# Graph attention layer on one core: edge rows behind tile 1, the first product split at token 256, and splits and output sums moved to later places

## The chip, the core and the metric

The kernel runs on one core of one Trainium2 chip, in float32 (matrix products in the fp32r form). The metric is the device time of one execution in microseconds (us); several executions are summarised by their median. Engines are named as in the profile: PE is TensorE (PEld its weight loads), DVE is VectorE, ACT is ScalarE, POOL is GpSimd, and SP is SyncE, whose queue (SPq) issues nearly all DMAs.

## The reference, cut to what matters

```python
# N=384 tokens, D=1024 features, H=16 heads of 64
h = maximum(layernorm(x), 0)
q, k, v = h @ wq.T + bq, h @ wk.T + bk, h @ wv.T + bv
q2, k2, v2 = q @ wiq.T + biq, k @ wik.T + bik, v @ wiv.T + biv      # split into 16 heads
mask = -inf; mask[src, dst] = softplus(edge_weight)[type - 1]       # 6528 edges, last one wins; diagonal filled
attn = softmax(q2 @ k2.T / 8 + mask)
out  = x + (attn @ v2 as N x 1024) @ wo.T + bo
```

## The kernel before, in words

**Precision scheme.** Each float32 operand is split into a high part (fp32r) and a low remainder. A product is three matrix products: hi x hi, hi x lo, lo x hi. For a weight this means two instructions per chunk of 128 x 1024: `split_hi` (L77, a copy on ACT) and `split_lo` (L82, a subtraction on DVE or POOL).

**Weight stream.** The weights come as 56 chunks, numbered by `w`: 0-7 are wv, 8-15 wq, 16-23 wiv, 24-31 wk, 32-47 alternate wiq and wik (one pair `p` holds two heads), 48-55 are wo. `W0` is 32. `load(w)` (L62-L65) issues the DMA of a chunk into a tile `raw`, and there are three such buffers (`bufs=3`), so chunk `w` takes the buffer of chunk `w-3` once both splits of that one have read it. The split pair lies in `whl`, four buffers.

**Order.** The whole order is written out by hand (`manual_schedule`): every engine executes its instructions in the order in which the Python code emits them, and semaphores are put in by the framework. SP issues DMAs in that order as well.

**Start.** The three token tiles of x, the edge rows `er`, and the first weights are loaded (L95-L106). Each x tile goes through statistics (`ln_bn`, L251, DVE; `ln_mean`), subtraction of the mean (`ln_sub`, L280 ACT, L282 POOL, L284 DVE), transposition on PE (`ln_transpose`, L292), and a split into hi and lo (`ln_hi` L298 ACT, `ln_lo` L303 DVE). Chunk 0 is split on POOL in halves (L344, L346). `key_rows` (L180) turns the edge rows into keys on POOL and stores them to DRAM (L185); `key_load` (L196) reads them back, broadcast. The product of chunk 0 (L414) takes all hi x hi first, then halves of the low terms.

**Projections.** `proj` (L405) makes vT, qT and kT, L503 makes the values; the edge mask is built beside them on DVE, POOL and by DMA.

**Attention.** `fill_qk` (L593) is a generator of the wiq and wik products: per chunk `w` eight blocks of three matmuls into `gps[w]`, and a head task `qk_head(w)` (L576) that is to load chunk `w+4`, split chunk `w+2`, and evict the product before (`qk_done`, L548: ACT L377, DVE L378, then four DMAs that stack the result into `qs`, L557-L560, or `ks`, L567; for `p` above 0 all four are on SP). The first 28 blocks are emitted ahead of the loop (`PRE`), so the heads of chunks 32 to 35 too, with `now[0]` at -1. Then a loop of 59 steps (L767): step `i` emits, between filler blocks, the scores of head-tile `i` (`do_S`, L694, PSUM tag `s` with two banks), the masked maximum of `i-1` (`do_ttr`, L700, DVE, which frees the bank), the exponential of `i-2` (ACT L704), the normalisation of `i-3` (DVE L708, POOL L709), the transposes of `i-5` (L714), the split of the probabilities of `i-6` (L723, L724), every third step the value product (L731) and its eviction (L741, L742, L746, L747), and last the head tasks. Below, S6 stands for the scores of step 6; S0 to S5 use pair `p=0`, S6 is the first that needs `p=1`.

**Output.** When `fill_qk` is used up, `fill_o` (L657) fills the steps with the output product: for each of six output blocks the first half over four wo chunks (`KH`), whose sum is added to the residual by `ysum` (L651, L654, DVE), then the second half. `wo_prep(k)` (L623) splits wo chunk `k` at the steps in `WSTEPS`; `OPOOL` names the chunks whose low part POOL makes.

The head task before the change, which the text below follows instruction by instruction:

```python
def qk_head(w):
    first = w - W0 < 3
    if not first:
        load(w + 4)
        split_hi(w + 2)
    if pendq:
        pendq.pop(0)()
    if 0 < w - W0 < NTAB:
        mask_select(w - W0)
    if first:
        split_hi(w + 2)
    split_lo(w + 2, nc.gpsimd if (w + 2) % 2 == PAR else None)
```

## Time and profile before

| | |
|---|---|
| median of 3 runs | 303.34 us (301.37 to 303.49) |
| profiled execution, its own time | 302.19 us |
| its span, first to last instruction | 300.5 us (1.7 us lie around it) |
| PE busy | 293.1 us, 98% of the span |
| DVE, ACT, POOL busy | 200.5, 154.9, 155.7 us |
| granted TensorE clock | 0.999 |

The page of the profile gives busy time per engine, the span in 40 slices, the DMA queues, the chain of waits that ended last, and the costliest groups of instructions. The timeline lists instructions in order of time: start, duration, engine, line, operation, output<-input, and in brackets the idle time ahead of it with what ended it. A PE instruction's end is modelled, so between two matmuls the distance of their starts is the safer measure: in this trace it is 173 ns for 384 columns, 120 ns for 256 and 227 ns for 512.

### The profile page before, as it was taken

The numbers are of one execution on the slowest core, as the hardware profiler recorded it, in microseconds if no ns is written. First come the engines' busy times: TensorE is split into PE (matmuls) and PEld (weight loads), VectorE is DVE, ScalarE is ACT, GpSimd is POOL, SyncE is SP. The second block draws the span as 40 slices with busy tenths as digits, with TensorE's granted clock in tenths as the row PEclk, the third lists the DMA queues.
The fourth block names the chain that finished last, engine by engine and source line by source line (L and its number), as shares of the span: only waits on it lengthen the run. The fifth ranks groups of instructions, "written<-read, shape, count | busy, mean of one in ns | idle before, by whom it ended". The sixth has DMA issues, their size and how long they took to land.

```text
span 300.5 us, 4961 instructions
## 1 busy us (share of the span) xinstructions
PE 293.1 (98%) x1649; PEld 276.1 (92%) x1649; DVE 200.5 (67%) x492; ACT 154.9 (52%) x289; POOL 155.7 (52%) x164
## 2 busy tenths in 40 slices
PE   7899999999999999999999999999999999999995
PEld 5699999999988889999999999999999998888884
DVE  2959986655956463788865576767576757696523
ACT  3874644333422213554325667777777767676310
POOL 5865766271555785730033737373746467566210
PEclk9999999999999999999999999999999999999999
DMA  7899754642686668475369997646565636910005
GB/s 233 284 297 381 281 164 171 228 143 70 217 238 224 193 217 242 142 274 198 115 169 244 217 221 173 166 127 180 155 170 139 174 81 174 381 41 0 2 0 209
DMA packets 22377, 55.12 MB, mean 183 GB/s; under 512 B 4816, under 2 KB 8400, under 8 KB 22352
## 3 DMA queue, kind: packets, MB, share of 16 engines
q1 hardware_dynamic: 19968, 52.42, 57.7%
q0 software_dynamic: 2064, 1.80, 2.0%
q10 hardware_dynamic: 320, 0.59, 0.8%
q8 instruction: 13, 0.21, 0.3%
q14 instruction: 12, 0.10, 0.1%
HBM read 40.39 MB, written 4.97 MB: 151 GB/s over the span
## 4 chain that ended last, share of the span: by engine, by line
PE 95%; DMA 2%; DVE 1%; ACT 0%; issue 0%; SPq 0%
PE g L369 21%; PE g L367 21%; PE g L368 21%; PE s L694 6%; PE a L731 6%; PE t L714 5%; PE s L369 2%; PE s L368 2%; PE s L367 2%; DMA g<-in_x_dram 2%; PE t L369 2%; PE t L367 2%; PE t L368 2%; PE g L414 1%; PE a L369 1%; PE a L367 1%
## 5 line engine op out<-in xcount | busy, mean ns | idle before, releaser
L367 PE MATMUL g<-g,whl 128*128 128x384 f32 x312 | 106.4, 341 | 0.0
L369 PE MATMUL g<-g,whl 128*128 128x384 f32 x312 | 104.5, 335 | 0.0
L368 PE MATMUL g<-g,whl 128*128 128x384 f32 x312 | 104.2, 334 | 0.0
L228 POOL DMA_INDIRECT tab<-val,idx x51 | 57.6, 1129 | 40.3 <-issue 11.3
L77 ACT ACTIVATE whl<-raw 128x1024 fp32r<-128x1024 f32 x51 | 53.4, 1051 | 31.7 <-PE g L369 20.1
L709 POOL TENSOR_TENSOR e<-e,s 128x384 f32<-128x384 f32 x48 | 39.2, 830 | 41.2 <-DVE s L708 32.9
L368 PEld LDWEIGHTS g<-g,whl 128*128 128x128 f32 x312 | 58.7, 188 | 0.0
L367 PEld LDWEIGHTS g<-g,whl 128*128 128x128 f32 x312 | 58.6, 188 | 0.0
L369 PEld LDWEIGHTS g<-g,whl 128*128 128x128 f32 x312 | 58.5, 188 | 0.0
L82 DVE TENSOR_TENSOR whl<-raw,whl 128x1024 fp32r<-128x1024 f32 x41 | 50.2, 1224 | 9.6 <-ACT whl L77 7.9
L82 POOL TENSOR_TENSOR whl<-raw,whl 128x1024 fp32r<-128x1024 f32 x11 | 26.5, 2412 | 35.6 <-ACT whl L77 31.8
L383 ACT ACTIVATE g<-f,bc 128x384 fp32r<-128x384 f32 x24 | 14.8, 618 | 53.1 <-DVE f L382 46.8
L704 ACT ACTIVATE e<-e,s 128x384 f32<-128x384 f32 x48 | 29.4, 612 | 13.0 <-DVE s L700 13.0
L724 DVE TENSOR_TENSOR pt<-t,pt 128x384 fp32r<-128x384 f32 x48 | 26.4, 550 | 13.9 <-ACT pt L723 13.3
L723 ACT ACTIVATE pt<-t 128x384 fp32r<-128x384 f32 x48 | 23.2, 484 | 13.9 <-PE t L714 13.3
L700 DVE CUSTOM_DVE_ANT_0 e<-s,ma 128x384 f32<-128x384 f32 x48 | 26.3, 550 | 2.0 <-PE s L694 1.8
L694 PE MATMUL s<-ks,qs 128*128 128x384 f32 x96 | 25.3, 344 | 0.3 <-DVE s L700 0.2
L714 PE MATMUL t<-ident,e 128*128 128x128 f32 x144 | 23.5, 271 | 0.0
L382 DVE TENSOR_TENSOR f<-g,rrow 128x384 f32<-128x384 f32 x24 | 13.3, 555 | 13.5 <-PE g L369 7.6
L714 PEld LDWEIGHTS t<-ident,e 128*128 128x128 f32 x144 | 18.8, 140 | 3.1
L378 DVE SCALAR_TENSOR_TENSOR nat<-g,bc,nat 128x384 fp32r<-128x384 f32 x16 | 9.9, 618 | 16.4 <-ACT nat L377 14.4
L731 PE MATMUL a<-pt,vhl 128*128 128x384 f32 x96 | 20.8, 351 | 0.0
(147 smaller groups left out, 414.8 us busy)
## 6 DMA issues: line engine op xcount, KB each, us to landing
ks<-nat SPq DMA_DIRECT2D x30, 192.0 KB
raw<-in_wv_dram SPq DMA_DIRECT2D x8, 512.0 KB
raw<-in_wq_dram SPq DMA_DIRECT2D x8, 512.0 KB
raw<-in_wiv_dram SPq DMA_DIRECT2D x8, 512.0 KB
raw<-in_wk_dram SPq DMA_DIRECT2D x8, 512.0 KB
raw<-in_wiq_dram SPq DMA_DIRECT2D x8, 512.0 KB
raw<-in_wik_dram SPq DMA_DIRECT2D x8, 512.0 KB
raw<-in_wo_dram SPq DMA_DIRECT2D x8, 512.0 KB
```

Of the source, the lines that this page charges most:

```text
L77: nc.scalar.activation(dst[0], raw[w], AF.Copy)
L82: (eng or nc.vector).tensor_tensor(lo, raw[w], hi.bitcast(F32), OP.subtract)
L228: nc.gpsimd.indirect_dma_start(out=tabs[c // RNG], out_offset=bass.IndirectOffsetOnAxis(ap=idx[:, c:c + 1], axis=0), in_=val[:, c:c + 1], ...
L367: nc.tensor.matmul(ps, lhi, rhi, start=first, stop=False)
L368: nc.tensor.matmul(ps, lhi, rlo, start=False, stop=False)
L369: nc.tensor.matmul(ps, llo, rhi, start=False, stop=last)
L694: nc.tensor.matmul(ps[:, :N], qs[:, o, t * 128:(t + 1) * 128], ks[:, o, s, :], start=(s == 0), stop=(s == 1))
L704: nc.scalar.activation(es[i], es[i], AF.Exp, bias=s[:, 0:1], scale=-1.0, accum_out=s[:, 1:2])
L709: nc.gpsimd.tensor_tensor(es[i], es[i], s[:, 2:3].to_broadcast([128, N]), OP.mult)
L714: nc.tensor.transpose(ps[:, k * 128:(k + 1) * 128], es[i][:, k * 128:(k + 1) * 128], ident)
L724: nc.vector.tensor_tensor(lo, pv, hi.bitcast(F32), OP.subtract)
L731: nc.tensor.matmul(ps[:, :N], vhl[:, k, p, 2 * o:2 * o + 2, :], pts[h][:, s, k, :], start=(k == 0 and s == 0), stop=(k == 2 and s == 1))
```

## The change

Five edits: the DMA of the edge rows goes behind x tile 1 instead of tile 0; `key_rows`, `load(2)` and the first `key_load`s are emitted behind the mean subtraction of tile 0; the hi x hi product of chunk 0 is done first for tokens 0-255 and then for 256-383; in the heads of chunks 35 and 36 the splits of chunks 37 and 38 are taken out and emitted some steps later (`defer`), while load and eviction stay; and `ysum` of the first half is emitted behind `do_ttr` of its step (`ysums`, `flush_y`), with wo chunk 4's low part on POOL.

```diff
     for t in range(NT):
         nc.sync.dma_start(xt[t], x[t * 128:(t + 1) * 128, :])
-        if t == 0:
+        if t == 1:
             nc.sync.dma_start(er, erows)
...
-    key_rows()
-    load(2)
-    for s in range(NTAB):
-        key_load(0, s)
     ln_bn(0, 0)
     ln_bn(0, 1)
     ln_mean(0)
     ln_sub(0, 0, 512, nc.scalar)
     ln_sub(0, 512, D, nc.gpsimd)
+    key_rows()
+    load(2)
+    for s in range(NTAB):
+        key_load(0, s)
     p0 = ln_transpose(0)
...
             if w == 0:
-                for a, b, ks in ((0, 0, range(KT)), (1, 0, range(4)), (0, 1, range(4)), (1, 0, range(4, KT)),
-                                 (0, 1, range(4, KT))):
+                al = (0, N)
+                for a, b, ks, (n0, n1) in ((0, 0, range(KT), (0, 256)), (0, 0, range(KT), (256, N)),
+                                           (1, 0, range(4), al), (0, 1, range(4), al), (1, 0, range(4, KT), al),
+                                           (0, 1, range(4, KT), al)):
                     for k in ks:
-                        nc.tensor.matmul(ps[:, :N], whl[0][a][:, k * 128:(k + 1) * 128], src[:, b, k, :],
-                                         start=(a == b == k == 0), stop=(b == 1 and k == KT - 1))
+                        nc.tensor.matmul(ps[:, n0:n1], whl[0][a][:, k * 128:(k + 1) * 128], src[:, b, k, n0:n1],
+                                         start=(a == b == k == n0 == 0), stop=(b == 1 and k == KT - 1))
...
+    defer = []
+
+    def qk_split(w):
+        split_hi(w)
+        split_lo(w, nc.gpsimd if w % 2 == PAR else None)
+
     def qk_head(w):
         first = w - W0 < 3
         if not first:
             load(w + 4)
+            if w - W0 < 5:
+                pendq.pop(0)()
+                defer.append((now[0] + 6 - w + W0, w + 2))
+                return
             split_hi(w + 2)
...
-    PAR, OPOOL, ODVE = 1, (2, 3, 6), (2,)
+    PAR, OPOOL, ODVE = 1, (2, 3, 4, 6), (2,)
...
+    ysums = []
+
+    def flush_y():
+        while ysums:
+            ysum(ysums.pop(0))
+
     def fill_o():
...
             if k == 0:
+                flush_y()
                 oacc[OT[a]] = bank("g")
             omm(*OT[a], k)
             if k == KH - 1:
-                ysum(a)
+                ysums.append(a)
...
             if k == KH:
+                flush_y()
                 oacc[OT[a]] = bank("gggss"[a])
...
         if 0 <= i - 1 < S:
             do_ttr(i - 1)
+        flush_y()
...
         run_tasks()
+        while defer and defer[0][0] <= i:
+            qk_split(defer.pop(0)[1])
```

## The prediction

> **What bounds the kernel now.** I read the page first, then the chain of waits, then the timeline of the three stretches that the edits touch.

> The page's busy times (engine, us, share, instructions):

> ```profile
> PE 293.1 (98%) x1649; PEld 276.1 (92%) x1649; DVE 200.5 (67%) x492; ACT 154.9 (52%) x289; POOL 155.7 (52%) x164
> ```

> PE sets the time; no edit takes a matmul away (one adds eight). So I listed the distances between matmul starts and looked for those above the usual one of the shape. Between 19 and 165 us there is none. Gaps are left in four places: before the first product (12.26 us); S3 (0.15 + 0.11 us) and S6 (0.23 + 0.07); S15 and S21 (0.22 each), where nothing is changed; S44 and S45 (0.40 + 0.11, 0.15 + 0.11). **All that the change can win lies here: 0.57 us at S3 and S6, 0.77 at S44 and S45, and what comes off the start.**

> The start. First lines of the chain of waits (start, us, what), then rows of the timeline:

> ```profile
> 1.72 5.41 DMA g<-in_x_dram
> 7.16 1.30 DVE lnt L251 x2
> 12.26 4.41 PE g L414 x24
> ```

> ```profile
> 11.51 0.66 PE L292 MATMUL a<-ident,g 128*128 128x128 f32 x4
> 12.20 0.60 ACT L298 ACTIVATE g<-a 128x512 fp32r<-128x512 f32 x1
> 14.20 2.41 POOL L82 TENSOR_TENSOR whl<-raw,whl 128x1024 fp32r<-128x1024 f32 x1
> ```

> Tile 1 of x is waited for until 7.16; PE's last transposes of tile 2 start at 11.51, and the product waits until ACT has evicted them. The third row is weight chunk 1's low part, done at 16.61, first needed by PE at 16.85.

> Around S3 and S6, the timeline by engine:

> ```profile
> 159.71 2.49 POOL L82 TENSOR_TENSOR whl<-raw,whl 128x1024 fp32r<-128x1024 f32 x1 [3.76 <-ACT whl L77]
> 162.35 1.06 ACT L77 ACTIVATE whl<-raw 128x1024 fp32r<-128x1024 f32 x1 [2.26 <-DMA raw<-in_wiq_dram]
> 163.32 0.56 ACT L377 ACTIVATE nat<-g,bc 128x384 fp32r<-128x384 f32 x1
> 164.45 1.21 DVE L82 TENSOR_TENSOR whl<-raw,whl 128x1024 fp32r<-128x1024 f32 x1
> 165.58 0.55 DVE L700 CUSTOM_DVE_ANT_0 e<-s,ma 128x384 f32<-128x384 f32 x1
> 162.88 0.53 SPq L65 DMA_DIRECT2D raw<-in_wiq_dram  x1
> 164.56 2.64 SPq L567 DMA_DIRECT2D ks<-nat  x4
> 166.19 0.62 PE L694 MATMUL s<-ks,qs 128*128 128x384 f32 x2
> 172.08 0.58 PE L694 MATMUL s<-ks,qs 128*128 128x384 f32 x2
> ```

> S3 (166.19) waits for a maximum that stands on DVE behind chunk 38's low part, and that behind ACT's chunk 38 high part, which waits for its weights. S6 (172.08) is another thing: the records of DMA completions show the second `ks` DMA of pair 1 complete at 171.99, and PE's wait for that semaphore end at 172.03.

> Around S44:

> ```profile
> 259.76 1.23 DVE L82 TENSOR_TENSOR g<-raw,g 128x1024 fp32r<-128x1024 f32 x1 [0.39 <-ACT g L77]
> 260.91 1.49 DVE L654 TENSOR_TENSOR g<-g,g 128x512 f32<-128x512 f32 x2
> 262.31 0.55 DVE L700 CUSTOM_DVE_ANT_0 e<-s,ma 128x384 f32<-128x384 f32 x1
> 262.92 0.62 PE L694 MATMUL s<-ks,qs 128*128 128x384 f32 x2 [0.23 <-DVE s L700]
> ```

> A low part and two output sums stand ahead of the maximum that frees S44's bank.

> [...] chunk 40's load, issued at 162.88 ahead of the `ks` DMAs, completes at 170.25, they at 171.04 and 171.99. [...] here L82 takes 2412 ns on POOL, 1224 on DVE[...].

> **The change, part by part.** Sums are against the profiled execution (span 300.5, its own time 302.19).

> *Edge rows and key_rows.* Without the edge rows' 128 small packets (3.25 to 3.9 us) ahead of it, tile 1 lands about 0.5 us earlier. Tile 2 keeps its place; it completed at 8.49, so its statistics (now 8.61) start 0.1 earlier and no more. `key_rows` (0.27 + 0.39 + 0.29 us on POOL) now comes behind tile 0's subtraction (ends 6.81) and the later edge rows (about 7.2): done by 8.3, about when tile 1's subtraction becomes ready. SP's queue behind its store holds `load(2)` (issued 7.15, now some 8.7) and the key loads; the store's packets moved at 10.25 to 11.25 behind 2.5 MB of x and weights, and still will, so completion (11.80, 12.83) stays. Cost nothing; without that cover, 1 us for chunk 2, whose low part is done at 18.4 and used from 21 us on.

> *Split at 256.* PE may start the first eight matmuls when tile 2's transposes are out: 11.51 - 0.1 + 4 x 0.109 = 11.86, not 12.26; ACT's evictions of tile 2 (to 12.7) are covered by 8 x 0.12 = 0.96 us of work. The 128-column matmuls cost between 67 ns (the line through 120, 173 and 227) and 109 (the transposes' distance)[...]. [...] But chunk 1's low part is ready at 16.61 less about 0.1[...]. **Part: -0.2 us**, from 0 (109 ns) to -0.35.

> *Deferred splits.* The head of chunk 35 runs ahead of the loop, so chunk 37 is due at the end of step -1 + 6 - 3 = 2; the head of chunk 36 runs at the end of step 1 (28 blocks ahead of the loop, then 7.9/3 a step), so chunk 38 is due at step 1 + 6 - 4 = 3. Gains: ACT's eviction of chunk 35 no longer stands behind L77 (1.06 us with its wait): 163.32 becomes about 162.65, where PE ends that product; DVE's maximum of S1 ends at 164.4, not 166.1. S3's 0.26 us goes.

> **The step that decides** is another instruction of the same head: `load(40)`. It stays at step 1 and needs chunk 37's buffer (three buffers, 40 - 3 = 37), and chunk 37 is now split after it. On SP it stands ahead of pair 1's `ks` DMAs. Before, POOL had done chunk 37 at 162.20 and SP passed at once. Now: ACT evicts chunk 35 (to 163.15), the exponential of S0 (to 163.75), chunk 37's high part (1.05, to 164.8), then POOL's low part (2.45, to 167.3). Load issued 167.35, first `ks` DMA about 168.0 instead of 164.56, though its data is ready at 163.8. The queue is empty by then, which gives much back: pair 0's four `ks` DMAs, issued from 155.03 on into an idle queue, had their second completion at 159.08, 4.05 us later. Chunk 40's load ahead of them (128 packets, 26 per quarter us, so 1.2 us, half of it before they start) adds up to 0.65. Second completion: 168.0 + 4.05 + 0.35 = 172.4, against 171.99. So S6 moves 0.35 to 0.4 later, and S3's and S6's 0.57 is replaced by a wait of about 0.9 us. **Part: +0.3 us.** Bounds: -0.57 if the load does not hold SP; +3.3 if the DMAs take 6.9 us as they did before (165.07 to 171.99, in a full queue). Chunk 37 itself is first used at 168.3, a us after its low part; chunk 38, done by 167.8, at step 7: nothing lost. Behind the `ks` DMAs on SP stand chunk 41's load and pair 2's `qs`, needed at S12 (185): covered.

> *Sums and wo chunk 4.* DVE loses 1.23 us; POOL takes 2.41 from 259.7 to 262.1 in an idle stretch of 3.5. The maximum for S44 then runs at 259.4: its 0.51 us goes. The sums of blocks 0 and 1 follow it, waiting for PE until about 262.3; then the probabilities' low part (0.55), L742 (0.55) and block 2's sum (0.7), which `flush_y` still puts ahead of the next maximum, because block 3 starts in the same step: that maximum ends near 264.8, S45 would be ready at 264.6. S45 keeps a wait of about 0.25 us. **Part: -0.4 us**, from 0 to -0.77.

> Sum: -0.2 + 0.3 - 0.4 = -0.3: 301.9 for the profiled execution, which lay 1.15 below the median; from the median **303.0 us**.

> **Rivals.** *A, the load does not hold the path* (POOL is through sooner, or the `ks` DMAs complete before 171.5): -0.2 - 0.57 - 0.5 = -1.3, **302.0**. For it: the queue is idle then. Against: load and `ks` DMAs are one queue, and POOL's 2.45 us can't start before ACT's. *B, slower: the held load makes S6 late.* From a completion 0.6 us above before's (172.6) on it eats the other two gains. At 174.0, midway to the full-queue time of 175.4, S6 is 2.0 later: -0.2 + 2.0 - 0.4 = +1.4, **304.7**. For it: completions of these DMAs spread over 3 us. Against: pair 0's 4.05. *C, the edits don't do what they say* (sums still ahead of S45's maximum, the split eaten by 109 ns): 0 + 0.3 - 0.1 = +0.2, **303.5**.

> **How the numbers follow.** Forecast 0.45, A 0.25, B 0.2, C 0.1. A measurement of this kernel can tell about 1%, 3 us: its runs alone spread over 2.1. All gaps together are about 2.5 us, so faster by 1% needs luck in the runs: 0.08. Slower by 1% needs B at its bound: 0.06. Range: A's lower end (302.0 less 0.8 for the runs' scatter) to B (304.7): 301.2 to 304.7.

> **What would show it.** Right: chunk 40's load issued near 167.3 and the `ks` DMAs behind it near 168; S3 without a gap, S6 with one of about 0.9 us; first product at 11.9 with sixteen short matmuls; S44 without and S45 with a small gap. Wrong: chunk 40 issued near 163 (A), the second `ks` DMA complete after 173.5 (B), or a new gap at chunk 37's first low matmul.

## The result, and the profile after

The change made the kernel slower, by a little under 1% and clear of the interval: 305.51 us median (304.03 to 305.88, 6 runs) against 302.71 us of the kernel before in the same comparison, ratio 1.0086 with a 95% interval of 1.0065 to 1.0107. A second comparison later gave 306.02 against 302.77 us, ratio 1.0117 (1.0082 to 1.0152). The forecast was 303.0 us with a range of 301.2 to 304.7, so both the value and the direction were wrong; what happened is rival B, and more of it than B had.

The profiled execution took 304.03 us (span 302.3; before 302.19 and 300.5). Line numbers shift in the changed kernel: scores are L714, the masked maximum L720, the output sum L666, the first product L416. The page's busy line for PE, which had 98%:

```profile
PE 292.8 (97%) x1657; PEld 276.7 (92%) x1657; DVE 200.0 (66%) x491; ACT 155.0 (51%) x289; POOL 158.5 (52%) x165
```

The position of PE at fixed points of the program (start of the named matmul, us) says where the 1.83 us between the two profiled executions arise:

| | before | after | difference |
|---|---|---|---|
| first product | 12.26 | 11.51 | -0.75 |
| chunk 1's first matmul | 16.50 | 16.21 | -0.29 |
| S0 | 160.85 | 160.56 | -0.29 |
| S5 | 169.61 | 169.05 | -0.56 |
| S6 | 172.08 | 174.34 | +2.26 |
| S43 | 260.46 | 262.76 | +2.30 |
| S45 | 265.24 | 267.06 | +1.82 |
| last matmul | 296.70 | 298.53 | +1.83 |

Three of the four parts gain about what was forecast (start 0.29, S3 0.27, S44 and S45 0.48). The start's 0.29 is one execution against one, and no larger than the scatter: in the nine profiles, here and below, that have the change's whole start, S0 lies between 160.34 and 161.39 us. One place, S6, loses 2.8 us. The timeline of PE and SP there:

```profile
166.79 0.33 SPq L65 DMA_DIRECT2D raw<-in_wiq_dram  x1
167.22 3.75 SPq L569 DMA_DIRECT2D ks<-nat  x4
174.34 0.59 PE L714 MATMUL s<-ks,qs 128*128 128x384 f32 x2 [2.88 <-DMA ks<-nat]
```

Chunk 40's load is issued at 166.79 (before 162.88) and the `ks` DMAs behind it from 167.22 on (before 164.56); S6 then waits 2.88 us for them. The chain of waits for this stretch (start, us, what) shows how the wait came about, from beginning to end:

```profile
163.32 0.96 ACT whl L77
164.28 0.07 issue
164.35 2.42 POOL whl L82
166.77 0.02 issue
166.79 0.33 SPq L65
...
167.73 6.51 DMA ks<-nat
174.25 0.09 issue
174.34 0.59 PE s L714 x2
```

Chunk 37's high part on ACT, its low part on POOL, then, 0.02 us after POOL is done, the load that was waiting for that buffer, then the DMA that stands behind the load. Of such a chain one reads the joints: POOL's end and SP's issue at the same instant point to SP's queue having been held by POOL; the first and the fourth experiment test it.

The chain's longest piece, 6.51 us for one `ks` DMA, can be read further. The trace records the completion of each such DMA in sixteen parts. Chunk 40's load completes fifteen of them by 170.81 and the sixteenth at 173.34; the second `ks` DMA, which S6 waits for, fifteen by 172.54 and the sixteenth at 174.25. An 8 KB packet that the profile calls an instruction packet (queue q14) runs from 167.85 to 169.51. From 169.51 on, eight of the load's 128 packets, one sixteenth, follow each other without a break until 171.98; all the others are through by 170.08. That the instruction packet held this sixteenth of the load back, and with it the last parts of the `ks` DMAs, is an estimate of mine from these times: the packet records do not name the DMA engine that moved a packet.

### The profile page after: what moved, and what is told of

Its sections match the earlier page's. It is cut to its first block, busy times and chain, and to the rows that moved or that the text cites. A ratio compares the mean times of both kernels' runs of the same rounds, so it can differ in the third digit from the quotient of the medians.

```text
span 302.3 us, 4981 instructions
## 1 busy us (share of the span) xinstructions
PE 292.8 (97%) x1657; PEld 276.7 (92%) x1657; DVE 200.0 (66%) x491; ACT 155.0 (51%) x289; POOL 158.5 (52%) x165
## 4 chain that ended last, share of the span: by engine, by line
PE 92%; DMA 3%; ACT 2%; POOL 1%; DVE 1%; SPq 0%; issue 0%
PE g L369 21%; PE g L367 20%; PE g L368 20%; PE a L751 6%; PE s L714 5%; PE t L734 5%; DMA ks<-nat 2%; PE s L368 2%; PE s L369 2%; PE s L367 2%; PE g L416 2%; PE t L369 2%; PE t L368 2%; PE t L367 2%; DMA g<-in_x_dram 1%; POOL whl L82 1%
## 5 line engine op out<-in xcount | busy, mean ns | idle before, releaser
L228 POOL DMA_INDIRECT tab<-val,idx x51 | 56.7, 1111 | 39.5 <-issue 11.1
L77 ACT ACTIVATE whl<-raw 128x1024 fp32r<-128x1024 f32 x51 | 53.5, 1051 | 29.2 <-PE g L369 18.1
L82 DVE TENSOR_TENSOR whl<-raw,whl 128x1024 fp32r<-128x1024 f32 x41 | 51.1, 1247 | 13.9 <-ACT whl L77 13.1
L729 POOL TENSOR_TENSOR e<-e,s 128x384 f32<-128x384 f32 x48 | 40.1, 847 | 35.1 <-DVE s L728 26.7
L82 POOL TENSOR_TENSOR whl<-raw,whl 128x1024 fp32r<-128x1024 f32 x11 | 26.4, 2400 | 41.2 <-ACT whl L77 37.5
L720 DVE CUSTOM_DVE_ANT_0 e<-s,ma 128x384 f32<-128x384 f32 x48 | 26.3, 549 | 5.8 <-PE s L714 5.6
L714 PE MATMUL s<-ks,qs 128*128 128x384 f32 x96 | 25.1, 342 | 2.9 <-DMA ks<-nat 2.9
L714 PEld LDWEIGHTS s<-ks,qs 128*128 128x128 f32 x96 | 17.2, 188 | 4.9 <-issue 3.2
```

The lines of the kernel that those rows point to most:

```text
L77: nc.scalar.activation(dst[0], raw[w], AF.Copy)
L82: (eng or nc.vector).tensor_tensor(lo, raw[w], hi.bitcast(F32), OP.subtract)
L228: nc.gpsimd.indirect_dma_start(out=tabs[c // RNG], out_offset=bass.IndirectOffsetOnAxis(ap=idx[:, c:c + 1], axis=0), in_=val[:, c:c + 1], ...
L714: nc.tensor.matmul(ps[:, :N], qs[:, o, t * 128:(t + 1) * 128], ks[:, o, s, :], start=(s == 0), stop=(s == 1))
L729: nc.gpsimd.tensor_tensor(es[i], es[i], s[:, 2:3].to_broadcast([128, N]), OP.mult)
```

## The experiments

T1 is the theory that chunk 40's load, held until chunk 37's buffer is free, holds SP's queue and with it pair 1's `ks` DMAs. T2 is the rival that the moved splits themselves are the harm. Each run was compared with runs of the kernel before on the same chip.

**The load behind the eviction.** One order swapped, in the head of chunk 36 alone:

```diff
         if not first:
-            load(w + 4)
+            if w - W0 != 4:
+                load(w + 4)
             if w - W0 < 5:
                 pendq.pop(0)()
+                if w - W0 == 4:
+                    load(w + 4)
```

> The change with one pair of instructions swapped: in the head of chunk 36 the eviction with its four ks DMAs stands ahead of the load of chunk 40. Theory T1 (the load, held until chunk 37's buffer is free, holds SP's queue and so the ks DMAs of pair 1): first ks DMA issued near 163.3 us, S6 without a gap near 171.4, the chunk 40 load still late near 166.8 but harmless; span about 299.4 us against 302.3 of the change and 300.5 of the kernel before, ratio to before about 0.996. Rival T2 (the moved splits themselves crowd ACT, DVE and POOL, or the ks DMAs are slow by themselves): S6 stays at 173.5 or later, span 301.8 or more, ratio above 1.004.

Measured: 301.26 us against 302.74, ratio 0.9942 (0.9922 to 0.9963), span 299.3. The timeline:

```profile
163.58 2.40 SPq L569 DMA_DIRECT2D ks<-nat  x4
166.96 0.33 SPq L65 DMA_DIRECT2D raw<-in_wiq_dram  x1
171.47 0.51 PE L717 MATMUL s<-ks,qs 128*128 128x384 f32 x2
```

The load is as late as in the change (166.96), but it holds nothing that is due; the splits are where the change puts them, and S6 has no gap. T2 falls.

**Without the deferral.** The change with the old head of `qk_head`.

> The change without the deferred splits; the edits of the start and of the output sums stay. T1 and T2 alike: all the loss is in the deferral, so S0 is 0.3 us earlier than before, S3 and S6 have the gaps of the kernel before (0.26 and 0.3 us), the end is 0.47 earlier still: span about 299.7, ratio about 0.9975. If the loss sits elsewhere (edge rows, sums on POOL): ratio above 1.0.

Measured: 301.39 us, ratio 0.9954 (0.9937 to 0.9971). So the loss lies in the deferral, and the deferral's own 0.57 us, once its order is mended, can't be told apart in the medians: the interval overlaps with that of the run above. The start's part was not seen in this profile: S0 comes at 160.99, not 0.3 us ahead of the 160.85 of before.

**The deferral alone**, in the kernel before.

> The kernel before with the deferred splits alone. T1 and T2: S3's gap goes, S6 waits some 3 us, span about 303.1, ratio about 1.010 to 1.012. If the start or the sums had their part in the loss: ratio below 1.006.

Measured: 307.2 us, ratio 1.0135 (1.0093 to 1.0177). In its profile (span 305.1) S6 waits 2.83 us for the `ks` DMAs, as forecast; but PE is 2.08 us late at S0 (162.93) already, which the expectation didn't have. The table by stage shows why (us; then busy time of PE, PEld, DVE, ACT, POOL; then the granted clock, DMA share, GB/s):

```profile
10.00:12.00 2.00, 1.31 (x10) 1.14 (x11) 1.93 (x5) 1.25 (x3) 2.00 (x3) 0.94 0.82 301
12.00:14.00 2.00, 2.00 (x9) 1.70 (x9) 2.00 (x4) 1.33 (x3) 2.00 (x3) 0.50 0.20 78
14.00:16.00 2.00, 2.00 (x10) 2.00 (x10) 2.00 (x5) 2.00 (x5) 1.27 (x3) 0.71 0.83 260
```

The TensorE clock was granted at half from 11.7 to 15.2 us. So this execution holds a fall of the clock at the start as well as S6's wait. That raised a question about the change: five of its first six executions had a mean granted clock of 0.994 and were 0.65 to 1.85 us longer than the profiled one, which had 1.0.

**A buffer of its own.** Chunk 40 goes into a tile that is free at that time; every instruction keeps the change's order.

```diff
+        if w == 40:
+            t = work.tile([128, 2, NT, N], F32R, tag="pt", name="raw")
+            raw[w] = t.bitcast(F32).rearrange("p a k n -> p (a k n)")[:, :D]
+        else:
+            raw[w] = wpool.tile([128, D], F32, tag="raw", name="raw", bufs=3)
```

> The change with chunk 40 loaded into a tile of its own (a free tile of the probabilities' size), every instruction in the change's order: the load has no buffer to wait for. T1: load issued near 162.2, first ks DMA near 163, S6 without a gap near 171.4, span about 299.4, ratio about 0.996, as in the swap. T2: S6 at 173.5 or later and span 301.8 or more, since order and splits are those of the change.

Measured: 300.83 us, ratio 0.992 (0.9891 to 0.9949), span 299.1:

```profile
161.68 0.53 SPq L69 DMA_DIRECT2D raw<-in_wiq_dram  x1
163.34 2.55 SPq L573 DMA_DIRECT2D ks<-nat  x4
171.23 0.51 PE L718 MATMUL s<-ks,qs 128*128 128x384 f32 x2
```

The order is the change's, only the buffer is free, and the 3 us are gone. With the swap this leaves T1 alone: neither the order nor the buffer does harm without the other. T1 says why the load and the `ks` DMAs start late; how long they then take is a further question, which the runs on chunk 40's load below take up.

**The change once more**, for the clock.

> The change itself once more, to see where the executions lose their time that are 1 to 1.8 us longer than the profiled one and have a mean granted clock of 0.994. T3 (the wait at S6, over 3 us long, lets the TensorE clock fall to half for some 3.4 us): the clock record of such an execution shows 0.5 just behind S6, near 175 us, and none at the start; median about 305.5. Rival T4 (the fall comes at the start, between the warm-up matmuls and the first product, as in the profile of the kernel with the deferred splits alone): 0.5 near 11 to 15 us.

Measured: 306.02 us, ratio 1.0117, all four executions at 0.994 or below. The profiled one (305.47 us, span 303.8) fell at S6. Its timeline and its table by stage:

```profile
174.26 0.59 PE L714 MATMUL s<-ks,qs 128*128 128x384 f32 x2 [3.02 <-DMA ks<-nat]
175.44 0.84 PE L734 MATMUL t<-ident,e 128*128 128x128 f32 x3
175.94 0.67 PE L367 MATMUL g<-g,whl 128*128 128x384 f32 x1
```

```profile
173.00:175.00 2.00, 0.74 (x4) 0.77 (x5) 0.12 (x1) 0.00 (x0) 0.06 (x1) 0.98 0.94 268
175.00:177.00 2.00, 2.00 (x9) 1.91 (x8) 0.68 (x4) 0.68 (x2) 0.82 (x1) 0.50 1.09 236
```

After a wait of 3.02 us the clock is at half from 174.91 for 3.41 us, and matmuls start 320 ns apart instead of 174. From S6 to S12 PE takes 14.65 us; in the first profile of the change, where the clock stayed up, 13.12. So the wait costs another 1.5 us on top of itself. The span confirms it: 303.76 - 302.32 = 1.44. T4 falls for this execution. For the other executions of the change with a low clock the place of the fall isn't recorded; but of 73 executions of the other runs here that load the edge rows as the change does and have no long wait at S6, only 2 have a mean clock of 0.994 or less, against 9 of the change's 10, which speaks for S6. The last section sets this wait beside the others.

**The evictions behind the splits.** Chunk 35's eviction and then chunk 40's load follow chunk 37's splits, so the `ks` DMAs find an idle queue and no load ahead.

> The change with chunk 35's eviction emitted behind chunk 37's splits at step 2, and chunk 40's load behind the eviction's four ks DMAs: these find an idle queue and no load ahead of them. It measures the disputed term by itself, the time from the first ks issue to the second completion. My term was 4.05 us on an idle queue. If the load ahead is what makes it 7.0 in the change: first issue near 165.5, second completion near 170, no gap at S6. If the ks DMAs are that slow by themselves: second completion near 172.5 and a gap of about 1 us.

Measured: one execution, 301.0 us, span 299.3:

```profile
164.62 2.41 SPq L569 DMA_DIRECT2D ks<-nat  x4
171.40 0.51 PE L716 MATMUL s<-ks,qs 128*128 128x384 f32 x2
```

The second `ks` DMA completes at 168.32, 3.70 us after the first issue (the third at 169.25). S6 has no gap. The `ks` DMAs by themselves are not slow, and on SP alone they are no slower than pair 0's 4.05 us on two queues.

**One step sooner.** `now[0] + 5 - w + W0` instead of 6.

> The change with both deferred splits one step sooner (steps 1 and 2), the load of chunk 40 still ahead: ACT makes chunk 37's high part before the first exponential. T1: POOL is through about 0.6 us sooner, so load and ks DMAs are issued 0.6 sooner and S6's gap is about 2.4 us instead of 3.0. T3: [...] no execution has a clock of 0.994 from it, and the median falls by more than 0.6, to about 303.3. Without T3: by 0.6, to about 304.9.

Measured: 302.35 us, ratio 0.9992 (0.9973 to 1.0011). Eleven of twelve executions have a clock of 0.999 or 1.0, as T3 says, but the rest went otherwise than expected: S6's wait is about 0.6 us, not 2.4, since the second `ks` DMA completes 5.9 us after the first issue (167.45, 173.38) and S4 and S5 come 0.63 and 0.75 us later, counted from S0. The timeline:

```profile
168.61 0.62 PE L714 MATMUL s<-ks,qs 128*128 128x384 f32 x2 [0.47 <-DVE s L720]
173.47 0.58 PE L714 MATMUL s<-ks,qs 128*128 128x384 f32 x2 [0.43 <-issue]
```

Sooner, chunk 38's low part stands ahead of the maximum that S4's bank waits for: S3's old stall has moved to S4. That the same load ahead costs 1.1 us less here than in the change (5.93 against 7.03) can be followed in the parts of the completions: fifteen parts of the second `ks` DMA take 5.57 us here and 5.32 in the change, but the sixteenth follows after 0.36 us and not after 1.71. The instruction packet runs here from 170.16 to 170.51 us, 3.14 us behind the load's issue (167.02); in the change it runs from 167.85, 1.06 us behind it (166.79). With S6's wait as short as that, the change costs nothing against the kernel before.

**Without the split at token 256**, on the kernel with chunk 40's own tile.

> The kernel with chunk 40 in a tile of its own, without the split of the first product at token 256 (eight matmuls of 384 columns as before). It parts the start's gain between the edge rows and the split. By my working the split starts the product 0.4 us sooner and costs 8 x 0.120 + 8 x 0.111 - 8 x 0.173 = 0.46 us more on PE: no net gain, so chunk 1 starts where it did (16.14 to 16.39) or 0.1 sooner, span 299.1, ratio about 0.992. If the split is what gains: chunk 1 starts at 16.5, span 299.4, ratio 0.993.

Measured: 301.22 us, ratio 0.9946 (0.9926 to 0.9966), span 299.1. The first product starts at 11.86 and chunk 1 at 16.12; with the split they start at 11.43 and 16.14:

```profile
11.86 4.42 PE L420 MATMUL g<-g,whl 128*128 128x384 f32 x24
16.12 0.34 PE L371 MATMUL g<-g,whl 128*128 128x384 f32 x1
```

The split gives 0.43 us and takes it back. In the change's trace the 128-column matmuls start about 112 ns apart, those of 256 columns 120: a matmul of a third of the 384 columns takes two thirds of the time (112 of 173 ns).

**Block 2's sum behind the maximum**, on the same kernel, with the split.

```diff
             if k == 0:
-                flush_y()
+                while ysums and ysums[0] <= a - 3:
+                    ysum(ysums.pop(0))
                 oacc[OT[a]] = bank("g")
```

> The kernel with chunk 40 in a tile of its own, and block 3's start in step 44 flushes only the sum whose bank it takes (block 0's, long done), so block 2's sum stays behind the maximum of step 44. By my reading of the change's trace block 2's sum is what still delays S45's bank: S45's gap of 0.16 and 0.11 us goes, span 298.85, ratio about 0.991. Rival: the maximum is late because of L762 and the probabilities' low part too; then the gap shrinks by less than half, span 299.0.

Measured: 301.08 us, ratio 0.9944 (0.9924 to 0.9964), span 298.85. The maximum now runs at once behind L767 and the sum after it:

```profile
262.60 0.56 DVE L725 CUSTOM_DVE_ANT_0 e<-s,ma 128x384 f32<-128x384 f32 x1
263.08 0.69 DVE L670 TENSOR_TENSOR g<-g,g 128x512 f32<-128x512 f32 x1
263.66 0.52 PE L719 MATMUL s<-ks,qs 128*128 128x384 f32 x2
```

S45's gap is gone, as expected; the 0.27 us show in the trace and not in the medians.

**Half of the load ahead.** In the change, 512 of chunk 40's 1024 columns are loaded ahead of the `ks` DMAs, the others behind them.

> The change with only half of chunk 40's load (512 of 1024 columns) ahead of the ks DMAs and the other half behind them; the held point is the same. It doses the disputed term. If the time from the first ks issue to the second completion, 7.0 to 7.2 us with the whole load ahead and 4.6 with none, grows with the bytes ahead: about 5.8, and S6's gap about 1.8 us instead of 3.0. If it is the hold and not the bytes: 7.0 and 3.0.

Measured: one execution, 304.74 us. First issue 167.38, second completion 173.44: 6.06 us.

```profile
166.94 0.33 SPq L66 DMA_DIRECT2D raw<-in_wiq_dram  x1
167.38 2.81 SPq L572 DMA_DIRECT2D ks<-nat  x4
173.53 0.87 PE L719 MATMUL s<-ks,qs 128*128 128x384 f32 x2 [1.92 <-DMA ks<-nat]
```

The 4.6 us of the expectation is the third `ks` DMA's time; the second's is 3.70. The table has, for the profiles that bear on this, the time from the first `ks` issue to the fifteenth and to the sixteenth part of the second completion, and the instruction packet of that stretch (us):

| load ahead | run | fifteen parts | all sixteen | instruction packet |
|---|---|---|---|---|
| none | evictions behind the splits | 3.69 | 3.70 | 169.19 to 169.52, behind them |
| none | the load behind the eviction | 4.32 | 4.47 | 168.69 to 169.54, behind them |
| half | this run | 4.19 | 6.06 | 168.90 to 169.75 |
| all | the change | 5.32 | 7.03 | 167.85 to 169.51 |
| all | the change once more | 5.42 | 7.17 | 167.62 to 169.44 |
| all | the deferral alone | 5.41 | 6.98 | 170.18 to 172.10 |
| all | one step sooner | 5.57 | 5.93 | 170.16 to 170.51 |

In the second row the queue was not idle, since chunk 39's load was under way until 165.08. Measured against the first row, the time to the fifteenth part grows with the bytes ahead: 0.5 us for half the load, 1.6 to 1.9 for all of it. The sixteenth part adds 1.6 to 1.9 us more in four of these profiles, 1.87 for half of the load and 1.57 to 1.75 for all of it, so it did not grow with the bytes. In each of the four, with an instruction packet of 0.85 to 1.91 us, one sixteenth of the load's packets starts within 0.01 us of the end of the instruction packet and runs behind all others. No experiment moved the instruction packet by itself, so that it is the cause was not shown; why it took so long in these four and 0.35 us one step sooner is open. Here the clock fell too (at 173.65, for 3.41 us), after a wait of only 1.92 us.

## Why the prediction was wrong, point by point

*What bounds the kernel* was right: PE, and gaps in few places. S15's and S21's gaps of 0.22 us stayed.

*Edge rows and the split at 256*: -0.2 forecast, -0.29 measured. Tile 1 completed at 5.36 instead of 7.14 in its profile, tile 2 at 8.00 instead of 8.49, so "no more than 0.1" for tile 2 was too little; the 128-column matmuls, which I had put below my upper bound of 109 ns, took about 112. The -0.2 between the bounds of 0 and -0.35 was an estimate of mine that no trace of before fixed. That the sum came out near is luck: the two errors offset each other, and what is left comes from the DMA order, not from the split.

*Deferred splits*: S3's gap went. The step that decides was named: `load(40)` waits for chunk 37's buffer and holds the `ks` DMAs. Its times were near: load 167.35 forecast and 166.79 measured, first `ks` issue 168.0 and 167.22. **The term that failed is the time from there to the second completion: 4.05 + 0.35 = 4.4 us, measured 7.03.** The 4.05, taken from pair 0, was not the fault: with no load ahead it is 3.70. The fault is the load ahead, put at 0.35 us because its 128 packets would pass at 26 per quarter us; it costs 7.03 - 3.70 = 3.3. Of these, 1.6 are the load itself: its packets pass at about 27 per half us from 168 to 169, and why at half the pace on a queue that had just been idle is not settled. The other 1.7 are the sixteenth part, which came late behind an instruction packet; the prediction took a DMA as one transfer and had no term for that.

Fifteen parts were there at 172.54, close to the 172.4 forecast, but that is luck too: the issue came 0.8 us sooner and the time was 0.9 longer than forecast. By this reckoning S6's wait would have been 1.2 us without the late part, and the change about level with the kernel before. My own bound (6.9 us from the second issue, in the full queue; the change has 6.5 so counted) held the truth, but I gave it to rival B with 0.2 and let the range end about midway to it.

*A second price was missing altogether.* Behind S6's wait of 3.02 us in the second profile of the change the clock stood at half for 3.41 us, which cost 1.5 us more. It fits the median, which lies 1.5 above the first profile. Nothing in the trace of before showed a wait of that length, and I did not price B's wait with it: 2.26 + 1.5 - 0.48 = 3.3 us over before, which is the difference of the two profiled spans (303.76 - 300.49 = 3.27), where B had 1.4.

*Sums and wo chunk 4*: -0.4 forecast, -0.48 measured, S45's rest of 0.26 us as described.

*Rival A* is what the swap, the own buffer and the late eviction make true: 302.0 forecast for it, 300.8 to 301.3 measured. *C* had no part beyond the split.

## What to carry to other kernels

When work is moved later, look at what stays behind in the old place: a load that reuses the moved work's input buffer now waits for it, and holds everything behind it on its queue (here the load from 162.88 to 166.79 us, and the first `ks` DMA behind it from 164.56 to 167.22). Price such a hold with the transfers' own times, with the bytes ahead of them, and not with a packet rate read elsewhere; and look at the parts of a completion: S6 waited for the last of sixteen, 1.71 us behind the fifteenth. TensorE's waits of 1.92 and 3.02 us here were followed by 3.41 us at half clock and so cost twice; those of 2.83 and 2.88 us were not.

## What the runs showed of the hardware that I had not expected

| profile | window | PE busy in it | PE idle in it | clock behind it |
|---|---|---|---|---|
| the change | 169.42 to 172.84 | 2.04 | 1.38 | full |
| the change | 172.84 to 176.25 | 1.91 | 1.50 | full |
| the deferral alone, S6 | 172.17 to 175.58 | 1.66 | 1.75 | full |
| the deferral alone, start | 8.33 to 11.74 | 1.53 | 1.88 | half |
| half of the load ahead | 170.23 to 173.65 | 1.50 | 1.91 | half |
| the change once more | 171.49 to 174.91 | 0.65 | 2.77 | half |

In these rows a window with 1.75 us idle or less is followed by full clock, and one with 1.88 or more by half; so are the windows at the kernel's end, with 3.01 us idle in the profile of before and 3.41 in the first of the change. In the first profile of the change a border of two windows cuts the wait of 2.88 us into 1.38 and 1.50; that it kept its clock for this reason is an estimate of mine from these few windows. No experiment moved a wait against the border, and the ends of PE's instructions are modelled, so the distance of 1.75 from 1.88 us is as good as that model.

Such falls are not the change's alone. Of 71 executions of the kernel before that were run beside the experiments, 13 have a mean clock of 0.994 or less, though the profile of before has no long wait at S6. Where they fall isn't recorded; the one profile with the old start that shows a fall (the deferral alone) has it at the start. Against the 2 in 73 named above, the new start may have made them rarer; that was not tried.

In one place of the change's trace POOL normalises while DVE subtracts a low part beside it, and both take longer:

```profile
165.85 1.99 DVE L82 TENSOR_TENSOR whl<-raw,whl 128x1024 fp32r<-128x1024 f32 x1 [0.81 <-ACT whl L77]
166.70 2.67 POOL L729 TENSOR_TENSOR e<-e,s 128x384 f32<-128x384 f32 x2
```

where 1.2 and 1.7 us are usual; of the two POOL instructions only the first, which lies beside L82, is long (1.83 us). Why they are longer there was not tested. Chunk 37's low part, on POOL until 166.77, took its usual 2.41 us, so this is no part of S6's wait.
